# A graph layer with experts: queries kept on chip, message sums in a ring of 12 tiles, a reordered first stage

## The chip, the core and the metric

The kernel runs on one core of a Trainium2 chip. The core has a matrix engine (PE; its weight loads are listed apart as PEld), a vector engine (DVE), an activation engine (ACT), a general engine (POOL), an engine that only issues transfers (SP), and 16 DMA engines [...]. The engines run side by side, each through its own instructions in order, and wait for each other through semaphores. The metric is the time on the device in microseconds (us); lower is better. Before the change the median of three runs is 1573.82 us (1571.39 to 1576.54).

## What is computed

The input is `x` (6250 nodes of 256 numbers) and 100,000 weighted edges, sorted by destination. Everything is float32.

```python
xn = layernorm(x)
# graph convolution, residual inside
deg  = segment_sum(edge_weight, dst) + 1;  dinv = rsqrt(deg)
agg  = segment_sum((dinv[src] * edge_weight * dinv[dst])[:, None] * (xn @ W)[src], dst)
h    = agg + (dinv * dinv)[:, None] * (xn @ W) + b
gnn  = relu(0.5 * (layernorm(h) * gamma + beta) + 0.5 * xn)
# linear attention, 8 heads of 32, over all nodes
q = elu(xn @ Wq.T) + 1;  k = elu(xn @ Wk.T) + 1;  v = xn @ Wv.T
mix = (q @ (k.T @ v) / (q @ sum(k))) per head, then @ Wproj.T + bproj
x = x + gnn + mix
# 16 experts, the best 2 for each node, hidden width 512
y = layernorm(x);  gate = y @ gate_w + gate_b
w, e = softmax and index of the 2 highest gates
moe = sum_k w[k] * (relu(y @ w1[e[k]] + b1) @ w2[e[k]] + b2)
out = x + layernorm(y + moe) * f_gamma + f_beta
```

The graph sum is linear, so the kernel sums the rows of `dinv * xn` over the edges first and multiplies each sum by `W` after it.

## The kernel before

Nodes lie in 49 tiles of 128 rows; `X`, all of them, stays on chip. Edges are cut into 782 chunks of 128. `gps_layer` loads the edges and `X`, checks that the destinations of every group of eight chunks lie in a known window of 128 nodes, and branches to `windowed_layer`, which is what runs here; the other branch is not taken.

**Setup** (lines 239 to 445). Local destinations and weights, which lie as rows of edges, are transposed on PE into columns `loc_t`, `w_t` (`columns`, line 357); sources follow as `src_t`. Degrees are counted by one-hot products: for each of four quarters of the columns DVE builds `lo1` (line 396) and `hw` (line 400), and PE adds 196 small products per quarter into `deg` (line 408). DVE then takes mean and variance of the 49 tiles (lines 423 to 426), and a chain of small steps gives `dinv` and the scale and shift of the table, `rsd` and `nmr` (lines 433 to 444). The table `dinv * xn` is written to `AGG` (49 tiles on chip, line 449; ACT line 454, DVE line 456) and from there to memory as `w_hs` (lines 459, 461).

**The woven part.** All that follows is one loop over slots (line 1109). In slot c, POOL gathers the 128 source rows of chunk c from `w_hs` by an indirect DMA (line 1114) into one of 12 rows buffers, DVE builds a weighted one-hot matrix `hot` (line 1118), and PE multiplies chunk c - 6 (`LAG = 6`, line 1127); at the end of each group of eight chunks DVE adds the result to the tile's sum in `AGG` (line 1135). Between these, the slot runs pieces of other work that a class `Weave` keeps in a queue: each piece is a generator that says after how many slots it wants to go on. So the order of PE, DVE, ACT and SP is written out by the slot numbers; POOL's order is made by the planner of the tile framework. The pieces are:

- `own_terms`: each tile's own row, the table times `dinv` in place (line 663).
- `attend(t)`, one tile every 2.1 slots from slot 0: transposes of `xn` (line 474), keys (line 511), elu on ACT and DVE (lines 494 to 496), and products of keys with `xn` collected in two banks over all tiles (line 518). `context` turns them into one 256 x 256 matrix `M`.
- `zeros`: fills the slots of the expert inputs and outputs in memory (`w_xslots`, `w_yslots`, two sets of nodes) with zeros, 1 MB a transfer (line 884).
- `residual(pair of tiles)`: transposes of `xn` and of the sums, queries (line 585), `W` (line 591), the denominator, `M` (line 623), both layernorms, gates (line 655). A pair starts when its sums are complete, 16 slots after the pair before it at the earliest.
- `route(z, n)`: for 11 groups of tiles (line 118; eight of the first set, of 36 tiles, three of the second, of 13) the two best experts and a place for every token. It starts `RES` = 28 slots after the last residual piece of its group started.
- `scatter`: the normalised tokens by indirect DMAs into `w_xslots` (line 864), 98 in all.
- `expert`: 121 blocks of 128 tokens. SP loads the block's weights in two parts (642 and 512 KB) and its tokens (128 KB); PE, ACT and DVE compute (lines 936 to 965); SP stores 128 KB. Blocks start every 8, then 6 slots in the first set, every 4 in the second, not before their route; weights have four places, two of them in `AGG`.
- `combine(pair)`: two gathers per tile from `w_yslots` (line 987), the weighted sum, the last layernorm, and the output, one of five buffers `h` (line 1009). A pair every 5 slots; the first set after its last block, the second after the last block of all.

A sum's place in `AGG` is used again after its residual: as homes of tokens, weights and gathered rows (lines 1042 to 1050). One core, one SP queue: its loads, stores, fills and outputs go out in program order.

Of the kernel before, what the change touches and what calls it, by code (L numbers as in the profile page):

```python
# [122 lines left out]
RES = 28  # L123
# [8 lines left out]
def load_rows(eng, t, a):  # L132

    n = (ER - 2) * EW
    eng.dma_start(t[:ER - 2, :], a[:n].rearrange("(p c) -> p c", p=ER - 2))
    eng.dma_start(t[ER - 2:ER - 1, :], a[n:n + EW].rearrange("(p c) -> p c", p=1))
    eng.dma_start(t[ER - 1:ER, :PADC], a[n + EW:].rearrange("(p c) -> p c", p=1))

# [21 lines left out]
def gps_layer(ctx: ExitStack, tc: tile.TileContext, x, src, dst, ew, **rest):  # L160
# [8 lines left out]
    loc_e, src_e, ew_e = rows3[:ER, 0, :], rows3[:ER, 1, :].bitcast(I32), rows3[:ER, 2, :]  # L169
    flag = top.tile([1, 1], I32, name="flag")  # L170
    with tc.tile_pool(name="chk", bufs=1) as cp, \
            tc.tile_pool(name="chk_ps", bufs=1, space=bass.MemoryType.PSUM) as cps:
# [7 lines left out]
        for t0 in range(0, NFULL, 8):  # L180
# [5 lines left out]
                       allow_small_or_imprecise_dtypes=True)  # L186
        v.tensor_tensor(loc_e.rearrange("p (j e) -> p j e", j=CPR),
                        dst_e.rearrange("p (j e) -> p j e", j=CPR),
                        lo[:, :, None].to_broadcast([ER, CPR, P]), op=OP.subtract)
        ends = cp.tile([ER, 2], F32, name="ends")  # L190
# [5 lines left out]
        one = cp.tile([ER, 1], F32, name="one")  # L196
        v.memset(one, 1.0)
# [7 lines left out]
    with tc.If(ok) as cmp:  # L205
        windowed_layer(tc, X, rows3, **rest)
# [11 lines left out]
def windowed_layer(ctx: ExitStack, tc: tile.TileContext, X, rows3, W, b, gamma, beta, wqT, wkvT, wprojT, bproj,  # L218
# [4 lines left out]
    loc_e, src_e, ew_e = rows3[:ER, 0, :], rows3[:ER, 1, :].bitcast(I32), rows3[:ER, 2, :]  # L223
# [16 lines left out]
    ident = one([P, P], "ident")  # L240
    make_identity(nc, ident)
# [12 lines left out]
    zero_b = one([P, 512], "zero_b", BF)  # L254
    v.memset(zero_b, 0.0)
    ones = one([P, P], "ones")
    v.memset(ones, 1.0)
    before = one([P, P], "before")
    v.tensor_scalar(before, iota_row, iota_p, None, op0=OP.is_gt)
# [4 lines left out]
    v.tensor_scalar(tok, tok, float(N), 64.0, op0=OP.is_ge, op1=OP.mult)  # L264
    eps_t = one([P, 1], "eps_t")
    v.memset(eps_t, EPS)

# [4 lines left out]
    v.memset(mv1, 1.0)  # L272
# [3 lines left out]
    v.memset(mv2, 1.0)  # L276
# [3 lines left out]
    v.memset(logits[:, NFULL, :], 0.0)  # L280
# [3 lines left out]
    v.memset(usual, 1.0)  # L284
# [3 lines left out]
    v.memset(ones3, 1.0)  # L288
    loc_t = one([P, NCA], "loc_t")
    w_t = one([P, NCA], "w_t")  # L290
    src_t = one([P, NCA], "src_t", I32)

# [38 lines left out]
    wkv_sb = weight(wkvT, 2 * D, "wkv_sb", part(2, 2 * D))  # L331
    wq_sb = weight(wqT, D, "wq_sb")
# [9 lines left out]

    with tc.tile_pool(name="deg", bufs=1) as sp, \
            tc.tile_pool(name="deg_ps", bufs=1, space=bass.MemoryType.PSUM) as sps:
        spread = sp.tile([16, 8, P], F32, name="spread")
        v.memset(spread, 0.0)
        for a in range(8):
            v.tensor_copy(spread[:, a, a * 16:(a + 1) * 16], ident[:16, :16])
# [7 lines left out]

        def columns(rows_e, outs):
            for h in range(2):
                tp = sps.tile([P, CPR // 2, ER], F32, name="tpe", bufs=2)
                for j in range(CPR // 2):  # L360
                    c0 = (h * CPR // 2 + j) * P
                    nc.tensor.transpose(tp[:, j, :], rows_e[:, c0:c0 + P], ident[:ER, :ER])
                for o, copy in outs:
                    copy(o.rearrange("e (p j) -> e j p", j=CPR)[:, h * CPR // 2:(h + 1) * CPR // 2, :], tp)

        columns(loc_e, [(loc_i, v.tensor_copy), (loc_t, nc.scalar.copy)])
        columns(ew_e, [(w_t, nc.scalar.copy)])
# [20 lines left out]

        deg = sps.tile([16, 3, 512], F32, name="deg")
# [3 lines left out]
        for c0 in range(0, NCA, C):  # L393
# [26 lines left out]
        for t in range(NT):  # L420
# [3 lines left out]
            if t:  # L424
                v.bn_aggr(mv1[:, t - 1, :], halves[t - 1])
# [1239 lines left out]
```

## Time and profile before

| | us |
|---|---|
| median of 3 runs | 1573.82 |
| the profiled execution | 1570.62 |
| its span, first to last instruction | 1568.8 |
| busy: PE, DVE, POOL, ACT | 1302.3, 1023.2, 959.7, 610.6 |
| granted PE clock, mean | 0.948 |
| moved by DMA | 360.96 MB, 230 GB/s on average |

The span has stages with different limits. Gathers start at 115.8 and the last one at 1232.0; the first combine's work on DVE starts at 1326, PE's last block ends about 1502, and the rest is the combines of the second set. A page line of section 5 gives a group of like instructions: how many, busy time and mean length of one, then the idle time of the engine just before them and what ended most of it. A line of the window view gives busy time and instruction count of each engine in a stretch. PE's instructions overlap in time, so starts, not lengths, say what one costs. DMA-issuing instructions of POOL count here as busy[...].

### The profile page before, as it was taken

What the parts mean: (1) busy time and instruction counts of PE and PEld (TensorE: products, weight loads), DVE (VectorE), ACT (ScalarE), POOL (GpSimd) and SP (SyncE); (2) the same over time, 40 slices, a digit from 0 to 9 for tenths busy, and PEclk for the clock granted to TensorE, in tenths of its full rate; (3) what the DMA queues carried; (4) which work ended last, traced back from release to release, by engine and by line L of the source; (5) the groups of instructions that cost most, each with busy time, mean ns of one, the idle gap of its engine ahead of it and who ended that gap; (6) DMA issues with size and microseconds to landing.
All of it is one profiled execution on the core that took longest, in us unless ns stands there. A gap on an engine that the chain in (4) does not pass through costs nothing.

```text
span 1568.8 us, 23681 instructions
## 1 busy us (share of the span) xinstructions
PE 1302.3 (83%) x6438; PEld 972.2 (62%) x6438; DVE 1023.2 (65%) x3578; ACT 610.6 (39%) x1542; POOL 959.7 (61%) x990
## 2 busy tenths in 40 slices
PE   2918999887678989899998989979999987878930
PEld 2817888565456767677675767757767754545620
DVE  7953345578664877758577685856685756889045
ACT  1044555454422424234342433423433443455421
POOL 0007777777777777777777777777777404752042
PEclk9999999999789999999998998989999998999975
DMA  8059993333356767678776757668877767999932
GB/s 235 2 205 374 385 372 99 104 104 104 115 195 215 252 214 252 213 265 270 254 252 208 249 177 255 220 226 267 273 251 253 245 203 261 360 382 345 364 112 71
DMA packets 173553, 360.96 MB, mean 230 GB/s; under 512 B 26305, under 2 KB 110604, under 8 KB 173402
## 3 DMA queue, kind: packets, MB, share of 16 engines
q1 hardware_dynamic: 125454, 230.28, 42.1%
q0 software_dynamic: 47712, 128.17, 25.8%
q8 instruction: 57, 0.93, 0.3%
q10 hardware_dynamic: 236, 0.80, 0.2%
q14 instruction: 94, 0.77, 0.2%
HBM read 283.60 MB, written 75.54 MB: 229 GB/s over the span
## 4 chain that ended last, share of the span: by engine, by line


## 5 line engine op out<-in xcount | busy, mean ns | idle before, releaser
L1114 POOL DMA_INDIRECT rows<-w_hs,src_t x782 | 759.1, 971 | 349.2 <-issue 183.3
L1127 PE MATMUL acc<-rows,hot 128*128 128x256 f32 x1564 | 473.2, 407 | 72.3 <-DMA rows<-w_hs,src_t 64.5
L1127 PEld LDWEIGHTS acc<-rows,hot 128*128 128x128 f32 x1564 | 271.9, 198 | 138.2 <-issue 43.3
L1118 DVE TENSOR_SCALAR hot<-iota_g,loc_t,w_t 128x128 f32<-128x128 f32 x782 | 255.7, 356 | 25.9 <-PE acc L1127 25.9
L987 POOL DMA_INDIRECT AGG<-w_yslots,slot_i x98 | 99.5, 1015 | 125.7 <-DMA w_yslots<-AGG 82.6
L864 POOL DMA_INDIRECT w_xslots<-AGG,slot_i x98 | 99.5, 1015 | 97.7 <-ACT AGG L940 51.2
L957 ACT ACTIVATE hT<-htp,early 128x128 f32<-128x128 f32 x300 | 85.7, 369 | 175.3 <-PE htp L952 141.8
L944 PE MATMUL hp<-early,AGG 128*128 128x512 f32 x300 | 145.7, 609 | 9.4 <-ACT AGG L940 8.5
L961 PE MATMUL yp<-early,hT 128*128 128x256 f32 x600 | 146.3, 388 | 1.4 <-ACT hT L957 1.2
L496 DVE SCALAR_TENSOR_TENSOR q<-e,q 128x256 f32<-128x256 f32 (+1 forms) x98 | 41.9, 427 | 146.4 <-ACT q L495 144.2
L961 PEld LDWEIGHTS yp<-early,hT 128*128 128x128 f32 x600 | 116.7, 196 | 28.8 <-ACT hT L957 7.8
L948 DVE COPY AGG<-hp 128x512 f32<-128x512 f32 x92 | 63.3, 688 | 86.1 <-PE hp L944 85.9
L944 PE MATMUL hp<-AGG 128*128 128x512 f32 x184 | 89.9, 611 | 8.2 <-ACT AGG L940 7.2
L952 PE MATMUL htp<-ident,AGG 128*128 128x128 f32 x484 | 75.4, 279 | 20.3 <-DVE AGG L948 13.8
L961 PE MATMUL yp<-AGG,hT 128*128 128x256 f32 x368 | 88.4, 383 | 0.8 <-ACT hT L957 0.8
L944 PEld LDWEIGHTS hp<-early,AGG 128*128 128x128 f32 x300 | 55.9, 192 | 53.3 <-issue 36.7
L302 ACT ACTIVATE sd<-mv,eps_t 128x2 f32<-128x2 f32 (+2 forms) x76 | 22.5, 297 | 168.9 <-DVE mv L297 133.3
L961 PEld LDWEIGHTS yp<-AGG,hT 128*128 128x128 f32 x368 | 69.8, 192 | 21.6 <-ACT hT L957 7.2
L957 ACT ACTIVATE hT<-htp,AGG 128x128 f32<-128x128 f32 x184 | 52.4, 367 | 69.9 <-PE htp L952 46.2
L952 PEld LDWEIGHTS htp<-ident,AGG 128*128 128x128 f32 x484 | 58.9, 143 | 33.4 <-DVE AGG L948 17.4
L1135 DVE SCALAR_TENSOR_TENSOR AGG<-acc,dinv,AGG 64x256 f32<-64x256 f32 x147 | 70.8, 482 | 11.5 <-PE acc L1127 8.5
L965 DVE TENSOR_TENSOR AGG<-yp,early 128x256 f32<-128x256 f32 x75 | 31.7, 422 | 68.2 <-PE yp L961 60.6
(259 smaller groups left out, 2144.7 us busy)
## 6 DMA issues: line engine op xcount, KB each, us to landing
early<-in_experts SPq DMA_DIRECT2D x75, 642.0 KB
early<-in_experts SPq DMA_DIRECT2D x75, 512.0 KB
AGG<-in_experts SPq DMA_DIRECT2D x46, 642.0 KB
AGG<-in_experts SPq DMA_DIRECT2D x46, 512.0 KB
w_xslots<-zero_b SPq DMA_DIRECT2D x16, 1024.0 KB
w_yslots<-zero_b SPq DMA_DIRECT2D x16, 1024.0 KB
AGG<-w_xslots SPq DMA_DIRECT2D x121, 128.0 KB
w_yslots<-AGG SPq DMA_DIRECT2D x121, 128.0 KB
```

Source lines behind the costliest of these rows:

```text
L496: v.scalar_tensor_tensor(q[:r], e[:r], 1.0, q[:r], op0=OP.min, op1=OP.add)
L864: i = nc.gpsimd.indirect_dma_start(out=xslots[z], out_offset=IndirectOffsetOnAxis(ap=slot_i[:r, t, k:k + 1], axis=0), in_=y[:r], in_offset ...
L944: nc.tensor.matmul(hp, xT[:, c, :], w1[:, c, :], start=(c == 0), stop=(c == 1))
L948: copy_h(h, hp)
L952: nc.tensor.transpose(tp[:, f, :], h[:, f * P:(f + 1) * P], ident)
L957: act(hT[:, f, :], tp[:, f, :], AF.Relu, bias=b1[:, f:f + 1], scale=1.0)
L961: nc.tensor.matmul(yp[:, :D], hT[:, f, :], w2[:, f, :], start=(f == 0), stop=(f == FJ - 1))
L987: nc.gpsimd.indirect_dma_start(out=got[i, k]()[:r], out_offset=None, in_=yslots[z], in_offset=IndirectOffsetOnAxis(ap=slot_i[:r, t, k:k + ...
L1114: nc.gpsimd.indirect_dma_start(out=hrows[c], out_offset=None, in_=hs, in_offset=IndirectOffsetOnAxis(ap=src_t[:, c:c + 1], axis=0))
L1118: v.tensor_scalar(hots[c], iota_g[:, group_of(c) % 2, :], loc_t[:, c:c + 1], w_t[:, c:c + 1], op0=OP.is_equal, op1=OP.mult)
L1127: nc.tensor.matmul(accs[g], hots.pop(c), hrows.pop(c), start=begin, stop=end)
L1135: v.scalar_tensor_tensor(AGG[p0:p1, t, :], acc[p0:p1, :], dinv[p0:p1, t:t + 1], AGG[p0:p1, t, :], op0=OP.mult, op1=OP.add)
```

## The change

**Queries with the keys.** `attend` multiplies `xn` by keys and queries in one 512-wide product, and the elu of both is done 512 wide on ACT. The queries stay on chip in `Q`, 49 tiles, which first hold the table on its way to memory. `residual` no longer makes queries nor transposes `xn`; it works on both tiles of a pair at once where it can.

**Sums in a ring.** `AGG` of 49 tiles is gone. A sum lives in one of 12 places: the first four tiles in the two `hT` buffers, the others in a ring of eight. `own_term(t)` reads the tile's table rows back from `w_hs` and scales them; it runs for one tile at a time, as places come free.

**First stage.** `ident`, `loc_t` and `w_t` move into `gps_layer`, ahead of the branch, and that block is ordered by hand. Memsets of constants move behind the one-hot loops (`constants`). The first quarter of the one-hot loop is cut in two. For 32 tiles ACT makes the sums for mean and variance (`two_sums`), DVE keeps 17. The fill of the first `w_xslots` moves ahead of the table. The table is written in 14 slots before slot 0, between the first attends.

**The schedule.** Attends start at slot -14, 2.3 slots apart before slot 0 and 3.6 after; residual pairs may follow at 10 slots; `RES` is 24; the last 30 blocks of the first set come every 5 slots; the other fills (`fill`, the old `zeros`) come every 8. The output of `combine` has three buffers, shared by name with other rows. By these rules the last residual piece starts at slot 791 (before 797), the last route at 815 (825), the first combine at 815 (831), the last expert block at 941 (965), and the combines of the second set at 959 (983).

The diff, cut to its core:

```diff
-RES = 28
+RES = 24
...
+def columns(nc, pool, ident, rows_e, o):
+    for h in range(2):
+        tp = pool.tile([P, CPR // 2, ER], F32, name="tpe", bufs=2)
+        for j in range(CPR // 2):
+            c0 = (h * CPR // 2 + j) * P
+            nc.tensor.transpose(tp[:, j, :], rows_e[:, c0:c0 + P], ident[:ER, :ER])
+        nc.scalar.copy(o.rearrange("e (p j) -> e j p", j=CPR)[:, h * CPR // 2:(h + 1) * CPR // 2, :], tp)
...
+            tc.tile_pool(name="chk_ps", bufs=1, space=bass.MemoryType.PSUM) as cps, by_hand(tc):
...
+        make_identity(nc, ident)
+        one = cp.tile([ER, 1], F32, name="one")
+        v.memset(one, 1.0)
+        scratch = cp.tile([ER, 1], F32, name="scratch")
+        nc.scalar.copy(scratch, one)
         v.tensor_tensor(loc_e.rearrange("p (j e) -> p j e", j=CPR),
                         dst_e.rearrange("p (j e) -> p j e", j=CPR),
                         lo[:, :, None].to_broadcast([ER, CPR, P]), op=OP.subtract)
+        columns(nc, cps, ident, loc_e, loc_t)
+        columns(nc, cps, ident, ew_e, w_t)
...
+    def constants():
+        v.memset(ones, 1.0)
+        v.tensor_scalar(before, iota_row, iota_p, None, op0=OP.is_gt)
+        v.tensor_scalar(tok, tok, float(N), 64.0, op0=OP.is_ge, op1=OP.mult)
+        v.memset(eps_t, EPS)
+        v.memset(mv1[:, NFULL, :], 1.0)
+        v.memset(mv2, 1.0)
+        v.memset(logits[:, NFULL, :], 0.0)
+        v.memset(usual, 1.0)
+        v.memset(ones3, 1.0)
...
+    wkq = part(2, 2 * D)
+    weight(wkvT[:, :D], D, "wk", wkq[:, :, :D])
+    weight(wqT, D, "wq", wkq[:, :, D:])
+    wv = weight(wkvT[:, D:], D, "wv", part(2, D))
...
+    for _ in fill(0, xslots[0]):
+        pass
...
+        v.tensor_copy(loc_i, loc_t)
...
+        def two_sums():
+            for t0 in range(0, SA, 8):
+                for t in range(t0, t0 + 8):
+                    act(sp.tile([P, D], F32, name="unread", bufs=2), X[:, t, :], AF.Identity,
+                        accum_out=sums_[:, t:t + 1])
+                act(minus[:, t0:t0 + 8], sums_[:, t0:t0 + 8], AF.Identity, scale=-1.0 / D)
+                for t in range(t0, t0 + 8):
+                    act(sp.tile([P, D], F32, name="unread", bufs=2), X[:, t, :], AF.Square,
+                        bias=minus[:, t:t + 1], accum_out=squares[:, t:t + 1])
...
+        for n in (C // 2, C // 2, C, C, C):
...
+                columns(nc, sps, ident, sf, src_t)
+                two_sums()
+            c0 += n
...
+        for t in range(SA, NT):
...
+    def table(t):
+        r = rows(t)
+        if t % 4 == 1:
+            act(Q[:r, t, :], X[:r, t, :], AF.Identity, bias=nmr[:r, t:t + 1], scale=rsd[:r, t:t + 1])
+        else:
+            v.tensor_scalar(Q[:r, t, :], X[:r, t, :], mv1[:r, t, 0:1], rsd[:r, t:t + 1],
+                            op0=OP.subtract, op1=OP.mult)
+        if t % TG == TG - 1:
+            t0 = t + 1 - TG
+            n = min(NFULL, t0 + TG) - t0
+            nc.sync.dma_start(hs[t0 * P:(t0 + n) * P, :].rearrange("(t p) c -> p t c", p=P), Q[:, t0:t0 + n, :])
+            if n < TG:
+                nc.sync.dma_start(hs[NFULL * P:, :], Q[:rows(NFULL), NFULL, :])
...
+        kq = bank("kq")
         for k in range(2):
-            nc.tensor.matmul(kp[:r, :D], xnT[:, k, :r], wkv_sb[:, k, :D], start=(k == 0), stop=(k == 1))
-        kf = mp.tile([P, D], F32, name="q", bufs=3)
-        elu1(kf, mp.tile([P, D], F32, name="e", bufs=2), kp[:r, :D])
+            nc.tensor.matmul(kq[:r], xnT[:, k, :r], wkq[:, k, :], start=(k == 0), stop=(k == 1))
+        e = mp.tile([P, 2, D], F32, name="two_a", bufs=2)
+        pos = mp.tile([P, 2, D], F32, name="two_b", bufs=2)
+        act(e[:r].rearrange("p a c -> p (a c)"), kq[:r], AF.Exp)
+        act(pos[:r].rearrange("p a c -> p (a c)"), kq[:r], AF.Relu)
+        kf = mp.tile([P, D], F32, name="row", bufs=3)
+        v.scalar_tensor_tensor(kf[:r], e[:r, 0, :], 1.0, pos[:r, 0, :], op0=OP.min, op1=OP.add)
+        v.scalar_tensor_tensor(Q[:r, t, :], e[:r, 1, :], 1.0, pos[:r, 1, :], op0=OP.min, op1=OP.add)
...
+    RING = 8
+    hTs = [wp.tile([P, F], F32, name=f"hT{j}") for j in range(2)]
+    ring = [wp.tile([P, D], F32, name=f"agg{j}") for j in range(RING)]
+    def agg(t):
+        return hTs[t // 2][:, t % 2 * D:(t % 2 + 1) * D] if t < 4 else ring[(t - 4) % RING]
+    begun, summed, read = set(), set(), set()
+    def own_term(t):
+        r = rows(t)
+        nc.sync.dma_start(agg(t)[:r], hs[t * P:t * P + r, :])
+        yield 4
+        nc.scalar.mul(agg(t)[:r], agg(t)[:r], dinv[:r, t:t + 1])
+        begun.add(t)
...
+        q8 = q.rearrange("p t c -> p (t c)").rearrange("p (h d) -> p h d", d=HEAD)
+        qk = two("qk", 1)
+        v.tensor_tensor(qk[:r0], q, ksum[:r0, None, :].to_broadcast([r0, n, D]), op=OP.mult)
+        den = mp.tile([P, 16], F32, name="den", bufs=2)[:r0, :8 * n]
+        v.tensor_reduce(den, qk[:r0].rearrange("p t (h d) -> p t h d", d=HEAD).rearrange("p t h d -> p (t h) d"),
+                        axis=AX.X, op=OP.add)
+        yield 1
+        v.tensor_scalar(den, den, 1e-6, None, op0=OP.max)
+        v.reciprocal(den, den)
+        v.tensor_mul(q8, q8, den[:, :, None].to_broadcast([r0, 8 * n, HEAD]))
...
+        agT = turned([agg(t)[:r0] for t in ts_], "two_a", 2)
+        for t in ts_:
+            summed.add(t)
+        yield 3
+        hp = bank("hp").rearrange("p (t c) -> p t c", t=2)
+        for i in range(n):
+            for k in range(2):
+                nc.tensor.matmul(hp[:r0, i, :], agT[:, k, i * P:i * P + r0], w_sb[:, k, :], start=(k == 0), stop=False)
+            add_bias(hp[:r0, i, :], 0)
+        h = two("h2", 2)
+        nc.scalar.copy(h[:r0], hp[:r0, :n, :])
...
+        qT = turned([Q[:r0, t, :] for t in ts_], "two_b", 2)
+        for t in ts_:
             read.add(t)
...
+            o = pool.tile([P, D], F32, name="row", bufs=3)
...
+    PRE = 14
+    at = -PRE
     for t in range(NT):
-        weave.add(int(pitch * t), attend(t))
-    at = int(pitch * NT) + 9
+        weave.add(int(at), attend(t))
+        at += 2.3 if at < 0 else 3.6
...
+    to_fill = [(0, yslots[0]), (1, xslots[1]), (1, yslots[1])]
+    fill_at = 4
+    for z, a in to_fill:
+        weave.add(fill_at, fill(z, a))
+        fill_at += 8 * ((MOST[z] + 8) // 8)
+    summed_at = {}
+    def sum_from(t):
+        weave.add(max(16 * t - 4, summed_at.get(t - RING, -4) + 1 if t >= 4 + RING else -4), own_term(t))
+    for t in range(4 + RING):
+        sum_from(t)
...
+                for t in range(t0, t1):
+                    summed_at[t] = at + 3
+                    if t + RING < NT and t >= 4:
+                        sum_from(t + RING)
+                at += 10
...
+            ready = max(last_at + RES, scattered - 2)
...
+            scattered = ready + 11 + 2 * (b - a) * slow
...
-                block = max(block + (4 if z else 8 if n < 3 else 6), ready)
+                block = max(block + (4 if z else 8 if n < 3 else 5 if flush else 6), ready)
...
+    slot = -PRE
     while slot < NCH + LAG or weave.steps:
+        for t in range(NT * (slot + PRE) // PRE, NT * (slot + PRE + 1) // PRE if slot < 0 else 0):
+            table(t)
         c = slot
-        if c < NCH:
+        if 0 <= c < NCH:
...
+                        v.scalar_tensor_tensor(agg(t)[p0:p1], acc[p0:p1, :], dinv[p0:p1, t:t + 1], agg(t)[p0:p1],
```

## The prediction

> **What bounds the kernel now.** I read the page first, then busy time by stage, then single engines in order of time. Page: busy tenths of POOL and DMA, and the costliest group.
>
> ```profile
> POOL 0007777777777777777777777777777404752042
> ...
> DMA  8059993333356767678776757668877767999932
> ...
> L1114 POOL DMA_INDIRECT rows<-w_hs,src_t x782 | 759.1, 971 | 349.2 <-issue 183.3
> ```
>
> POOL shows a steady 7 from slice 4 to 30; it is full, as its timeline shows (start, length, idle before it):
>
> ```profile
> 352.98 0.94 POOL L1114 DMA_INDIRECT rows<-w_hs,src_t  x1 [0.30 <-issue]
> 354.23 0.94 POOL L1114 DMA_INDIRECT rows<-w_hs,src_t  x1 [0.30 <-issue]
> ...
> 1257.54 0.96 POOL L864 DMA_INDIRECT w_xslots<-AGG,slot_i  x1 [0.30 <-issue]
> 1309.68 0.96 POOL L864 DMA_INDIRECT w_xslots<-AGG,slot_i  x1 [51.18 <-ACT AGG L940]
> ```
>
> 0.94 of work and 0.30 between: 1.25 us for every indirect DMA. Counting gathers in this view, gather 0 starts at 115.8, gather 639 at 1030.9 and 781, the last, at 1232.0. Up to gather 639 there are 72 scatters too, so 711 DMAs in 915.1 us, 1.287 us each. That stretch is POOL's. Busy time of PE, PEld, DVE, ACT, POOL by stage, then clock, DMA share, GB/s:
>
> ```profile
> 83.00:116.00 33.00, 6.83 (x24) 5.41 (x24) 18.16 (x75) 15.59 (x33) 0.19 (x1) 1.00 0.66 227
> ...
> 1031.00:1244.00 213.00, 202.90 (x944) 152.56 (x943) 137.13 (x462) 81.58 (x216) 151.00 (x155) 0.98 0.79 262
> 1244.00:1326.00 82.00, 64.38 (x267) 41.91 (x265) 46.20 (x184) 34.29 (x90) 20.49 (x20) 0.94 0.69 233
> 1326.00:1452.00 126.00, 106.22 (x405) 67.26 (x406) 111.65 (x306) 62.83 (x181) 66.66 (x66) 0.96 0.97 350
> 1452.00:1502.00 50.00, 49.12 (x205) 33.03 (x204) 4.67 (x11) 23.70 (x67) 0.00 (x0) 1.00 0.85 311
> 1502.00:1569.00 67.00, 3.09 (x16) 2.17 (x14) 38.49 (x108) 10.01 (x24) 27.02 (x26) 0.56 0.29 83
> ```
>
> From 1031 to 1244 PE and POOL are about equally full. 1244 to 1326 is full nowhere. From 1326 DVE and DMA are full (first combines), then PE (last blocks), then DVE (last combines). PE's timeline there gives the price of an expert block:
>
> ```profile
> 1458.04 0.38 PE L936 MATMUL xtp<-ident,AGG 128*128 128x128 f32 x2
> 1458.26 0.60 PE L952 MATMUL htp<-ident,AGG 128*128 128x128 f32 x4
> 1458.94 1.98 PE L944 MATMUL hp<-AGG 128*128 128x512 f32 x4
> 1460.76 1.89 PE L961 MATMUL yp<-early,hT 128*128 128x256 f32 x8
> 1462.48 0.38 PE L936 MATMUL xtp<-ident,AGG 128*128 128x128 f32 x2
> ```
>
> From start to start 4.44 us. The starts also price single matmuls: 1.82 for four of 512 columns, 0.215 for one of 256, 0.11 for one of 128. The setup before gather 0, in order of time:
>
> ```profile
> 73.55 1.44 PE L417 MATMUL deg<-zero_b 128*16 128x504 bf16 x3
> ...
> 92.66 9.46 DVE L456 TENSOR_SCALAR AGG<-X,mv,rsd 128x256 f32<-128x256 f32 x29
> ...
> 115.81 1.12 POOL L1114 DMA_INDIRECT rows<-w_hs,src_t  x1 [103.20 <-issue]
> ```
>
> [...]
>
> **Part 1, setup.** Edge transposes before the branch: loc_e is ready at 7.1; ACT needs 8.0 (its sixth DMA issue ends at 6.5, table load 1.28), four copies of 0.8 end at 11.2; the flag's matmul waits on PE behind the fourth group: flag some 0.9 late. In exchange DVE reaches the one-hot loops at 17.8 (0.57 cast, four of 0.28, 3.8 for the thirds, from 12.3) instead of 25.4. Two half chunks cost 5.8 each (16 x 0.10 + 24 x 0.174, half of the elements, same fixed part) for one of 8.6; so chunk 2 ends at 38.0. Then PE's 196 small matmuls are the bound, 9.64 each: 38.0 + 3 x 9.64 + 1.44 = 68.3 (before 75.0). DVE now has 17 instead of 49 row statistics: four chunks end at 56.3, constants 1.2, bias thirds 2.7, 17 x 0.39: 67.2. ACT's 64 sums start after src_t at 30.9: [...] I take under 68. Then as before deg sums, dps and dinv: 1.94 + 5.0 (87.7 to 92.75), nmr at 75.3 instead of 92.75: 17.4 gained.
> The table stage: before 23.1 from nmr to gather 0. Now 14 slots with the first attends among the tables: par and memsets first 1.4, 37 x 0.33 on DVE, four attends' 8 x 0.43, waits for ACT's Exp and Relu about 2: last store issued at 19.5, landing and start 6 (before, 106.3 to 115.8 behind more traffic): 25.5. **Gather 0 at 101, gain 15.** The 11 fills of the first xslots (1 MB per 2.8 us) run from 31 to 64 in an idle DMA: nothing.
>
> **Part 2, slots 0 to 635.** POOL's count of DMAs is the same: 1.287 each. Attends: PE 0.22 + 1.72 + 0.86 per 3.6 slots plus 0.43 = 1.21 per slot, under POOL's. Without that cover (fewer slots) it would be PE's. Slots 171 to 237, residual pairs every 10 slots: before a pair cost DVE 9.8 (51.6 busy in 312 to 376, less 0.42 per slot, 3.1 pairs); five pairs of 256-wide operations become 512-wide, two elu go: about 8.2, so 1.24 per slot with hot and sums, just under. LAG leaves six slots of cover. The 49 table reads (128 KB, 6.4 MB in all) lie beside DMA at 0.65 to 0.7; ACT waits if one lands later than four slots, 5 us, and behind it stand ACT's copies of xT and hT, for which PE waits. On SP a read waits for PE to have turned the ring tile's last content, three slots earlier in the order, and expert loads stand behind it. I take 0, from -5 to +12.
>
> **Part 3, slots 635 to 788.** PE: 153 x 0.43 + 29 blocks x 4.11 (starts in PE's timeline from 1110 on, without waits: yp 1.73, hp 1.72, htp 0.44, xtp 0.22) + 10 tiles x 3.35 (three pairs of transposes 0.66, hp and mix with bias 1.16 each, gl 0.37; before 4.43, with qp 0.86 and a fourth pair) + 2 for routes = 221. The same sum for before gives 217 where 213 passed, so 216 against 218.5 (1025 to 1243.5): **-2.5**. Spacing 5 instead of 6 means that 29 of 30 blocks of the first set are done or under way, not 26.
>
> **Part 4, slots 788 to the first combine.** By the schedule's arithmetic the last residual moves from slot 797 to 791, its route from 825 to 815, the combines from 831 to 815, the last block's load from 965 to 941. Before: 82.5 us from 1243.5 to the first combine's DVE work at 1326: PE work 46, 12 of waits, and then POOL: five scatters of the last route stood ahead of the first combine gathers, at 1309.7 to 1314.7, landing at 1326. In the changed kernel's order 15 combine gathers stand ahead of those six scatters, and the stores they read are issued at slot 796. So: 5 blocks and three tiles, 31, the same 12, five slots 6: 49. **-33**. What is late next is the last scatter, behind one freed gather tile; the blocks that need it load from slot 829.
>
> **Part 5, to PE's end.** Before: 18 combine pairs of DVE 6.7 us (five slots, 1.34 per slot) to slot 926, then 1.11 per slot (4.44 / 4) to 978: 179 by this sum, 176 measured. Now 90 x 1.34 + 44 x 1.11 = 170, and the last route's DVE work (some 5) falls inside. DMA: 31 loads x 1.41 MB + 14 MB in 172 us is 335 GB/s, under the 350 measured. **-4.** Ring of three output rows instead of five: DVE reuses one after 10 us; an output queued behind one block's 1.15 MB at 350 GB/s lands in some 5. Hidden; without that up to 20. **Last 67 us unchanged.**
>
> Sum: -15 + 0 - 2.5 - 33 - 4 = -54.5 against the profiled 1570.6 (span 1568.8), which lies 3.2 below the median of 1573.8: **1519 us.**
>
> **Rivals.** (a) The combines start earlier but the tail does not shrink: DMA at 0.97 and DVE at 89% already fill 1326 to 1502, and the last scatters now queue behind gathers. For it: those shares; against: 2 to 3 fewer loads left. Then Part 4 gives some 12 and Part 5 nothing: 1545. (b) Part 1's ACT sums, or tables mixed with attends, eat the setup's gain and the rest holds: 1534. (c) The middle gains too, since fills hold DMA for 60 us instead of 90 and PE is lighter: at 1.26 per DMA 711 x 0.027 = 19 less, 1500, and down to 1490 with the tail's stalls. (d) Slower: ACT waits in order for each tile's table read. 49 reads; from 59 / 49 = 1.2 us lost to POOL at each, all gain is gone; at 1.3 us it is 1519 + 64 = 1583. Against: six slots of cover, DMA at 0.65. That the change does nothing is no rival: slots and counts differ in the built order.
>
> **Chances.** Forecast 0.55 (its own range 1502 to 1536), (a) 0.25, (b) within the forecast's upper edge 0.05, (c) 0.08, no change 0.02, (d) 0.05. A measurement of this kernel tells 0.3%. Faster 0.93, same 0.02, slower 0.05. The range leaves out (d), the far end of (a) and half of (c): 1496 to 1556.
>
> **What would show it.** nmr near 75 and gather 0 near 101; gather 635 near 1010; the last gather near 1225; combine gathers ahead of the last six scatters, DVE's first combine near 1274; PE's last block near 1447. Wrong if ACT shows waits on the ring's tiles of several us, if accumulating ACTIVATEs take over 0.6 us, or if PE idles in the last blocks.

## The result, and the profile after

The changed kernel takes 1549.3 us (1545.9 to 1551.4) beside 1575.2 us (1571.4 to 1579.0) for the kernel before, ratio 0.983, 95% interval 0.980 to 0.986: 26 us faster, where 54.5 were forecast. The time lies inside the widest range given (1496 to 1556) and outside the forecast's own (1502 to 1536). The profiled spans are 1547.3 and 1568.8, 21.5 apart, since the profiled execution of the kernel before, 1570.6, lay ahead of its median. From the gathers in POOL's timelines and from PE's last block, by stretch:

| stretch | before | after | forecast | measured |
|---|---|---|---|---|
| span's start to gather 0 | 115.8 | 107.6 | -15 | -8.2 |
| gather 0 to 635 | 907.7 | 915.4 | 0 | +7.7 |
| gather 635 to 781, the last | 208.5 | 220.3 | -2.5 | +11.8 |
| gather 781 to PE's end | 273.6 | 240.9 | -37 | -32.7 |
| PE's end to the span's end | 63.2 | 63.1 | 0 | -0.1 |

The forecast cut the third and the fourth stretch at slot 788, which is where PE's last product of gathered rows ends: 1243.7 before, 1260.5 after. Cut there, the third measures +17.3 (220.2 to 237.5) and the fourth -38.2 (261.9 to 223.7). So the setup fell short by 7 us, the next stretch by 8, the third by 20, and the fourth came as forecast. The page of the changed kernel, busy tenths and the gathers' group:

```profile
POOL 1017777777777777777777777777667734753042
...
DMA  9789933333345766677887878768878868899932
...
L1163 POOL DMA_INDIRECT rows<-w_hs,src_t x782 | 762.2, 975 | 354.1 <-ACT two_a L552 89.7
```

POOL's row of sevens is as long as before, but has two sixes in it (slices of 38.7 us, 1083 to 1161 us), where it had none: POOL waits there. Its timeline: gather 0, the first combine gather, the last two combine gathers ahead of the last route's scatters, and the first and last of those:

```profile
107.56 1.15 POOL L1163 DMA_INDIRECT rows<-w_hs,src_t  x1 [89.72 <-ACT two_a L552]
...
1280.83 0.98 POOL L1025 DMA_INDIRECT Q<-w_yslots,slot_i  x1 [10.29 <-DMA w_yslots<-Q]
...
1310.09 1.07 POOL L1025 DMA_INDIRECT Q<-w_yslots,slot_i  x1 [4.61 <-DVE xn L1036]
1311.47 0.95 POOL L1025 DMA_INDIRECT Q<-w_yslots,slot_i  x1 [0.30 <-DVE over L845]
1313.71 1.00 POOL L911 DMA_INDIRECT w_xslots<-Q,slot_i  x1 [1.29 <-issue]
...
1320.86 1.59 POOL L911 DMA_INDIRECT w_xslots<-Q,slot_i  x1 [0.30 <-issue]
```

The order is the one forecast: 15 combine gathers ahead of six scatters. Busy time by stage of the changed kernel (PE, PEld, DVE, ACT, POOL, then clock, DMA share, GB/s):

```profile
1023.00:1243.00 220.00, 207.84 (x940) 153.88 (x940) 128.38 (x399) 65.41 (x193) 153.36 (x158) 0.98 0.84 284
1243.00:1484.00 241.00, 210.96 (x850) 138.70 (x848) 165.45 (x523) 112.46 (x322) 88.41 (x87) 0.96 0.86 309
...
1325.00:1430.00 105.00, 86.03 (x327) 55.31 (x326) 94.02 (x260) 52.79 (x153) 55.94 (x56) 0.95 1.00 369
1430.00:1485.00 55.00, 52.77 (x219) 35.25 (x217) 12.07 (x32) 26.87 (x76) 0.00 (x0) 1.00 0.79 283
```

And the kernel before, over the same two stretches (gather 635 to 781, and on to PE's end):

```profile
1023.50:1232.00 208.50, 195.37 (x898) 145.44 (x896) 133.69 (x434) 73.96 (x197) 156.04 (x160) 0.98 0.78 260
1232.00:1505.00 273.00, 234.21 (x953) 154.12 (x952) 173.67 (x553) 130.25 (x361) 88.08 (x87) 0.96 0.84 300
```

Add the two rows of each kernel, and call PE's busy time its work and the rest its waits: PE has 429.6 us of work in 481.5 before, 418.8 in 461 after. The 20.5 us gained from gather 635 to PE's end are 10.8 of work, from the lighter residuals (their queries' products, busy for 11.4 us there before, are gone), and 10 of waits. What else the rows show is that work changed sides: the first stretch got 12 us of PE more, the second 23 less. In the first stretch PE's yp matmuls, eight to a block, count 168 before (21 blocks) and 208 after (26).

### The profile page after: what moved, and what is told of

It reads as the page before. It is cut to its first block, busy times and chain, and to the rows that moved or that the text cites. A ratio compares the mean times of both kernels' runs of the same rounds, so it can differ in the third digit from the quotient of the medians.

```text
span 1547.3 us, 22816 instructions
## 1 busy us (share of the span) xinstructions
PE 1312.2 (85%) x6144; PEld 930.1 (60%) x6144; DVE 975.0 (63%) x3338; ACT 530.6 (34%) x1417; POOL 967.1 (63%) x999
## 5 line engine op out<-in xcount | busy, mean ns | idle before, releaser
L1025 POOL DMA_INDIRECT Q<-w_yslots,slot_i x98 | 99.4, 1015 | 141.8 <-issue 81.1
L994 ACT ACTIVATE hT<-htp,early 128x128 f32<-128x128 f32 x296 | 84.5, 368 | 205.6 <-issue 130.1
L981 PE MATMUL hp<-early,Q 128*128 128x512 f32 x296 | 143.2, 607 | 5.6 <-ACT Q L977 4.7
L998 PEld LDWEIGHTS yp<-early,hT 128*128 128x128 f32 x592 | 116.9, 198 | 32.7 <-ACT hT L994 10.8
L985 DVE COPY Q<-hp 128x512 f32<-128x512 f32 x92 | 63.4, 689 | 113.7 <-PE hp L981 113.0
L911 POOL DMA_INDIRECT w_xslots<-Q,slot_i x98 | 99.6, 1016 | 46.8 <-issue 37.1
L549 PE MATMUL kq<-early,xnT 128*128 128x512 f32 (+1 forms) x196 | 98.5, 627 | 4.3 <-ACT xnT L545 4.3
L981 PE MATMUL hp<-Q 128*128 128x512 f32 x188 | 92.4, 615 | 10.1 <-ACT Q L977 9.1
L989 PE MATMUL htp<-ident,Q 128*128 128x128 f32 x484 | 74.7, 278 | 21.4 <-DVE Q L985 17.8
L998 PE MATMUL yp<-Q,hT 128*128 128x256 f32 x376 | 91.6, 388 | 0.4 <-ACT hT L994 0.3
L998 PEld LDWEIGHTS yp<-Q,hT 128*128 128x128 f32 x376 | 72.9, 195 | 19.6 <-ACT hT L994 5.2
L1185 DVE SCALAR_TENSOR_TENSOR agg<-acc,dinv,agg 64x256 f32<-64x256 f32 x135 | 65.0, 482 | 28.6 <-PE acc L1176 25.9
```

Source lines behind the costliest of these rows:

```text
L549: nc.tensor.matmul(kq[:r], xnT[:, k, :r], wkq[:, k, :], start=(k == 0), stop=(k == 1))
L911: i = nc.gpsimd.indirect_dma_start(out=xslots[z], out_offset=IndirectOffsetOnAxis(ap=slot_i[:r, t, k:k + 1], axis=0), in_=y[:r], in_offset ...
L981: nc.tensor.matmul(hp, xT[:, c, :], w1[:, c, :], start=(c == 0), stop=(c == 1))
L985: copy_h(h, hp)
L989: nc.tensor.transpose(tp[:, f, :], h[:, f * P:(f + 1) * P], ident)
L994: act(hT[:, f, :], tp[:, f, :], AF.Relu, bias=b1[:, f:f + 1], scale=1.0)
```

## The experiments

In the table the times are medians, the ratio is to the kernel before on the same chip; stretches are from one profiled run each, as above (that of e2 was the fastest of its four runs, 1555.5, that of e8 the slowest of its 18, 1575.3). Each text set off below was written ahead of its run.

| kernel | us | ratio (95%) | gather 0 | 0 to 635 | 635 to 781 | 781 to PE's end |
|---|---|---|---|---|---|---|
| e1_old_schedule | 1554.1 | 0.987 (0.985 to 0.990) | 107.4 | 909.9 | 204.3 | 266.5 |
| e2_flush6 | 1559.5 | 0.992 (0.990 to 0.993) | 106.0 | 914.6 | 203.0 | 266.2 |
| e3_warm | 1544.7 | 0.981 (0.979 to 0.983) | 103.3 | 915.6 | 218.6 | 241.5 |
| e4_spread | 1537.6 | 0.978 (0.975 to 0.982) | 106.1 | 914.1 | 220.1 | 234.1 |
| e5_stats_dve | 1558.3 | 0.990 (0.987 to 0.993) | 117.0 | 911.3 | 220.4 | 243.4 |
| e6_no_mix | 1541.3 | 0.980 (0.976 to 0.984) | 101.8 | 914.2 | 218.9 | 242.1 |
| e7_warm_spread8 | 1531.7 | 0.972 (0.969 to 0.976) | 104.3 | 915.0 | 220.3 | 228.1 |
| e8_before_flush5 | 1568.9 | 0.997 (0.996 to 0.998) | 116.3 | 906.7 | 222.4 | 265.3 |
| d1_res28 | 1550.0 | 0.985 (0.982 to 0.987) | 108.1 | 912.6 | 217.3 | 247.3 |
| d2_no_mix_spread8 | 1528.4 | 0.971 (0.969 to 0.973) | 102.2 | 912.4 | 220.3 | 226.6 |

**What the schedule is worth.** Two theories: the slots set the time (as the prediction reckoned), or PE's work and its waits do, whichever side of the last gather a block falls on. First both numbers of the schedule back:

```
-RES = 24
+RES = 28
...
-    ... 8 if n < 3 else 5 if flush else 6), ready)
+    ... 8 if n < 3 else 6), ready)
```

> The changed kernel with two numbers of the schedule as before: RES 28 instead of 24, 6 slots instead of 5 between the blocks of the first set's last phase. By the slot arithmetic the first combines go back from slot 815 to 831 and the last block's load from 941 to 965, as in the kernel before; all else stays. Theory W (from gather 635 to PE's end the time is PE's work, 421 us in the changed kernel and 430 before, plus what PE waits, 40 and 50; the schedule only decides on which side of the last gather a block falls): gather 635 to 781 goes back from 220 to about 208, the stretch after it grows by about as much, and the whole is 6 to 14 us slower than the changed kernel, 1555 to 1563. Theory S (the prediction's Parts 4 and 5: the 37 us are due to the earlier slots): the whole is 30 to 37 us slower, 1579 to 1586.

Then the spacing alone (the second of these edits):

> The changed kernel with only the spacing of the first set's last blocks back at 6 slots. The first combines start at slot 827 instead of 815, the last block's load at 961 instead of 941. Theory W: PE's five blocks are taken out of the stretch between gather 635 and 781, which shrinks from 220 to 207 to 210, and put behind it; the whole moves by less than 6 us, 1545 to 1555. Theory S: the combines start 12 slots later and the whole is 20 to 25 us slower, 1570 to 1575. Both expect six scatters of the last route ahead of all combine gathers again.

And the spacing alone in the kernel before, the other way round (6 to 5):

> The kernel before with one number changed: 5 instead of 6 slots between the blocks of the first set's last phase. The first combines move from slot 831 to 825, the last block's load from 965 to about 951. Theory W (PE's work and waits): about five blocks more fall between gather 635 and 781, which takes 8 to 14 us longer, and the stretch behind it gets shorter by that and up to 8 us more: 1566 to 1575 against 1574. Theory S (the slots set the time): 12 to 20 us faster than before. Rival: slower by 3 to 8 us, since the combines' gathers collide with more loads.

Undone, the two cost 5 us (e1) and the spacing alone 10 (e2), not the 30 and more of the slot theory. e1's 5 is just under its range of 6 to 14; e2's 10 is outside of the 6 expected, on the side of the slot theory but half of it. That e1, which undoes more, loses less goes with its shorter way to gather 635 (909.9 us). Set alone into the kernel before, the spacing gains 5 (inside the range of work and waits), and lengthens 635 to 781 by 14 there, as it shortens it by 16 and 17 when it is taken out: that stretch follows the number of blocks in it. The stages of e1:

```profile
1017.00:1222.00 205.00, 190.27 (x852) 140.44 (x851) 121.63 (x379) 58.64 (x165) 154.85 (x161) 0.97 0.80 270
1222.00:1488.00 266.00, 226.55 (x933) 149.22 (x931) 171.04 (x540) 120.94 (x348) 88.34 (x87) 0.97 0.86 308
```

416.8 of work in 471: the work of the changed kernel with the waits (54) of the kernel before. What the waits are, the first combine shows. In the kernel before, in e1 and in e2 the last route's scatters stand ahead of the first combine gathers on POOL; DVE, in order, waits for those gathers, and PE for DVE. DVE's first combine in the kernel before and in e1, then PE's waits for DVE behind gather 781 in the kernel before, in e1 and in the changed kernel (us in total, times, the longest):

```profile
1321.23 1.00 DVE L998 SCALAR_TENSOR_TENSOR xn<-AGG,w,xn 128x256 f32<-128x256 f32 x2 [9.59 <-DMA AGG<-w_yslots,slot_i]
1305.05 0.49 DVE L1036 SCALAR_TENSOR_TENSOR xn<-Q,w,xn 128x256 f32<-128x256 f32 x1 [9.71 <-DMA Q<-w_yslots,slot_i]
...
PE htp L952 <- DVE AGG L948: 13.8, 8, 8.8
PE htp L989 <- DVE Q L985: 19.3, 11, 9.9
PE htp L989 <- DVE Q L985: 6.6, 3, 2.8
```

So the combine gathers that come ahead of the scatters are worth the 10 us of waits, and the residuals' edits the other half of the gain.

**The waits that are left.** If DVE holds PE while it does the first combines, stretching them over the blocks behind should free PE:

```
-        at += 5
+        at += 7 if t0 < CUT else 5
```

> The changed kernel with 7 instead of 5 slots between the combine pairs of the first set (their end at slot 934 instead of 900, still ahead of the second set's combines at 959). Theory: between 1281 and 1430 DVE is at 125 of 149 us with combines and makes PE wait some 25 us (for Q from ACT and DVE), while from 1430 to 1485 DVE has 12 of 55 and PE 53: spread over the blocks, DVE no longer holds PE, PE's end moves from 1484 to 1466 to 1476, the whole is 8 to 18 us faster, 1531 to 1541. Rival 1: that stage is DMA's (share 1.00 from 1325 to 1430), so PE waits for its loads anyway: within 4 us. Rival 2: later combines keep the x and got tiles longer and end behind the last block: slower by 3 to 10 us.

12 us faster than the changed kernel; PE ends at 1474.3, within the range. PE's work stays (417.5 in 454.1 from gather 635 on), its waits fall from 42 to 37, and the stretch behind gather 781 loses 7 of the 12; most of the rest lies ahead of gather 781, where the edit does nothing and executions differ. With 8 slots and an attend-free table stage (d2_no_mix_spread8, below) the stage in which DMA had a share of 1.00 reads:

```profile
1325.00:1430.00 105.00, 99.37 (x402) 65.57 (x402) 72.22 (x200) 59.31 (x167) 45.77 (x48) 0.99 1.03 397
```

PE 99 instead of 86, DVE 72 instead of 94, and DMA moves 397 instead of 369 GB/s: a share of 1.00 was not the most that it moves. (This kernel is 8 us ahead; eight us earlier, from 1317, it reads 96, 72 and 388.) Spreading the combines moves their transfers too, so the edit alone doesn't part DVE from DMA. The waits from 1281 to 1430 do, first those of the changed kernel, then those of d2:

```profile
ACT sd L318 <- DVE mv L313: 38.9, 17, 6.2
PE hp L981 <- ACT Q L977: 11.1, 9, 2.2
PE xtp L973 <- DMA Q<-w_xslots: 1.0, 1, 1.0
...
ACT sd L318 <- DVE mv L1017: 8.5, 9, 1.4
PE hp L981 <- ACT Q L977: 3.1, 7, 0.8
```

In the changed kernel PE waits 1.0 us for a transfer. It waits for ACT's copies of the blocks' tokens, and ACT, in order, for DVE's statistics in the combines. So DVE holds PE, in part through ACT, and the DMA half of rival (a) falls.

**The setup.** PE's timeline of the changed kernel among the tables: attends 0, 1 and 2.

```profile
78.72 0.69 PE L518 MATMUL tp<-ident,early 128*128 128x128 f32 x2 [2.64 <-ACT early L540]
79.96 3.78 PE L549 MATMUL kq<-early,xnT 128*128 128x512 f32 x4 [0.55 <-ACT xnT L545]
83.53 0.63 PE L518 MATMUL tp<-ident,early 128*128 128x128 f32 x2
85.66 3.78 PE L549 MATMUL kq<-early,xnT 128*128 128x512 f32 x4 [1.50 <-ACT xnT L545]
...
90.89 1.98 PE L549 MATMUL kq<-early,xnT 128*128 128x512 f32 x4 [0.29 <-ACT xnT L545]
```

The first two kq (keys and queries) take 3.78 us, the third 1.98: the first two, with idle times of 2.64 and 0.55 us and of 1.50 us just before them, ran at about half rate. DVE stands behind them, its remaining tables behind each attend's sums:

```profile
84.89 0.42 DVE L555 SCALAR_TENSOR_TENSOR row<-two_a,two_b 128x256 f32<-128x256 f32 x1 [1.83 <-ACT two_b L553]
...
90.60 0.42 DVE L555 SCALAR_TENSOR_TENSOR row<-two_a,two_b 128x256 f32<-128x256 f32 x1 [1.78 <-ACT two_b L553]
```

Three experiments: PE kept busy ahead of them (heat(n) is n bf16 matmuls of 512 columns on zeros, whose result nobody reads), no attend among the tables at all, and the sums on ACT undone.

```
+        heat(4)
         dps = sps.tile(...)
...
+        heat(8)
         act(sdeg, dps, AF.Sqrt, ...)
```

> The changed kernel with 12 extra bf16 matmuls of 512 columns on zeros whose result nobody reads: 4 ahead of the degree sums' transposition, in PE's idle 70.4 to 72.4, and 8 behind it, in its idle 76.1 to 78.7. In the changed kernel the first two attends' four kq matmuls take 3.78 us each instead of the 1.98 of the later ones. Theory: PE runs at half rate after idling, and this holds the tables back, because the tables stand behind the attends on DVE: kq at about 2.0 to 2.6 in both, gather 0 at 104 to 106 instead of 107.6, the whole 2 to 3.5 us faster. Rival: the table stage is held by the stores' landing or by ACT: gather 0 within 0.7 us of 107.6, the whole unchanged.

```
-    at = -PRE
+    at = 0
...
-        at += 2.3 if at < 0 else 3.6
+        at += 3.15
```

> The changed kernel with no attend among the tables: all 49 start from slot 0 on, every 3.15 slots, so that the last one and the residuals come in the same slots as before. Tables alone: DVE 37 x 0.33 from 78.7 on, last store issued near 92, gather 0 at 97 to 100 (107.6 in the changed kernel). Theory: then PE sets slots 0 to 155, (0.22 + 1.82 + 0.86 + 3.15 x 0.43) / 3.15 = 1.35 us per slot instead of POOL's 1.26: gather 150 at about 300 to 306 against some 300 in the changed kernel, so that nothing is left of the earlier start: the whole from 2 us faster to 8 us slower. Rival: POOL holds its 1.26 us and the whole gains what gather 0 gains, 8 to 10 us.

```
-                two_sums()
...
-        for t in range(SA, NT):
+        for t in range(NT):
...
-        v.tensor_scalar(mv1[:, :SA, 0], minus, ...)
-        v.tensor_scalar(mv1[:, :SA, 1], squares, ...)
```

> The changed kernel without the sums on ACT: all 49 row statistics on DVE again, 0.39 us each, 32 more than in the changed kernel, 12.5 us. DVE reaches the degree sums at about 79.9 instead of 70.5 (2.9 us of the 12.5 go into its wait for PE there), so nmr at 86 to 87 instead of 77.2 and gather 0 at 116 to 118. Theory: POOL is full from gather 0 to 635, so the setup carries through one to one: the whole 8 to 11 us slower than the changed kernel, 1557 to 1561. Rival: the attends' matmuls, not POOL, set the first 160 slots, and absorb half of it: the whole 3 to 6 us slower.

With PE busy both kq take 1.98 and gather 0 comes at 103.3:

```profile
79.06 1.98 PE L549 MATMUL kq<-early,xnT 128*128 128x512 f32 x4 [0.80 <-ACT xnT L545]
80.88 0.38 PE L518 MATMUL tp<-ident,early 128*128 128x128 f32 x2
83.20 1.98 PE L549 MATMUL kq<-early,xnT 128*128 128x512 f32 x4 [1.94 <-ACT xnT L545]
```

That is 4.3 us ahead of the changed kernel and 2.7 ahead of e2 and e4, which have the changed kernel's setup unaltered (e7, with the same extra matmuls, has 104.3); the whole is 4.6 faster, though the intervals (0.979 to 0.983 and 0.980 to 0.986) still touch. Without attends among the tables gather 0 comes at 101.8 (97 to 100 expected) and the whole is 8 us faster. Here my expectation was wrong and its rival right: PE was to set 1.35 us per slot from then on, but gathers 100 to 200 came every 1.32, scarcely slower than in the changed kernel (132.5 us instead of 131.8), so little was given back. The sums on ACT are worth 9 us, as much as the whole gain of the setup: without them gather 0 is at 117.0, later than in the kernel before, and of these 9.4 us 9.0 are left at the end. The theory was right.

**Both ends together:**

> The extra matmuls of e3_warm and the first combines every 8 slots (e4_spread had 7) together. The two act at the two ends of the kernel; if they add up, 1.5 to 4.6 us of the first and 10 to 14 of the second: 1530 to 1537. If 8 slots are one too many, because the second set's gathers then wait behind the first set's last ones: 1537 to 1545.

> The changed kernel with e6_no_mix and 8 slots between the first combines together. e6_no_mix was 8 us faster than the changed kernel and the spacing 12 to 13 (e4_spread, e7_warm_spread8 less e3_warm); they act at different ends, so if they add up 1527 to 1532, and if not 1533 to 1540.

> Attends from slot 0 on and 8 slots between the first combines, a third time. Beside the changed kernel on the second chip it was 29 us faster. Where the kernel before takes 1574: 1525 to 1532, ratio 0.969 to 0.974.

d2_no_mix_spread8 is e6_no_mix with 8 slots between the first combines: 1528.4 us, 21 faster than the changed kernel and 46 than the one before. The 8 of e6 and the 13 between e3 and e7 (the same matmuls without and with 8 slots) make 21: they add up. e7's own 1531.7 lies in its first range. Eight slots alone were not run. e10 is the same kernel as d2, on another chip (below).

**The 7.7 us before gather 635.** They sit in two places: gathers 200 to 300 took 162.9 us instead of 157.6, and 500 to 635 207.3 instead of 203.3. For the second the routes' position was suspected, for the first the residuals' spacing:

```
-RES = 24
+RES = 28
```

```
-                at += 10
+                at += 10 if t0 < 4 else 14
```

> The changed kernel with RES 28 instead of 24 alone: every route, its scatters and blocks four slots later after its residuals, the first combines at slot 819 instead of 815. From gather 0 to 635 e1_old_schedule (RES 28) took 909.9 us, e2_flush6 (RES 24) 914.6, the changed kernel 915.4, the kernel before 907.7. Theory: the earlier routes put their DVE chains right behind the residuals', PE waits for them and then runs at half rate, and that is some 5 of the 7.7 us that the changed kernel lost before gather 635: 909 to 911 here, the whole 3 to 6 us faster than the changed kernel. Rival: the four slots come back in the tail as 4 to 5 us, the whole within 2 us.

> The same with RES 28. If the routes' position is worth what e9_res28 is to show, 3 to 6 us faster than e10_no_mix_spread8, 1522 to 1528; if it comes back in the tail, within 2 us of it.

> The changed kernel with 14 instead of 10 slots between the residual pairs from the third on, where they catch up with the gathers (slots 191 to 240; before: 16). Theory: DVE at 0.9 to 0.95 there lengthens POOL's own DMAs (mean of gathers 200 to 249 1.025 us in the changed kernel, 0.971 before): the mean falls to 0.96 to 0.99, gather 200 to 300 takes 158 to 160 instead of 162.9, the whole 2 to 4 us faster. Rival: it is the route behind them, not their spacing: no change within 1.5 us.

These, and e10_no_mix_spread8, landed on a chip on which the kernel before itself took 1780 us, so their times can't be set against the runs above. Repeated with the changed kernel beside them:

> The changed kernel itself, as the measure for the three beside it, since the last four ran where the kernel before took 1780 us instead of 1574. If the chip is like the first one: 1545 to 1553 against 1571 to 1577, gather 0 to 635 in 914 to 916 us.

> RES 28 alone in the changed kernel, once more. Theory (the earlier routes cost PE waits before gather 635): gather 0 to 635 in 909 to 911, the whole 3 to 6 us faster than c1_after. Rival: the four slots come back in the tail, within 2 us.

> 14 instead of 10 slots between the residual pairs from the third on, once more. Theory: mean of gathers 200 to 249 falls from 1.025 to 0.96 to 0.99 us, gather 200 to 300 takes 158 to 160, the whole 2 to 4 us faster than c1_after. Rival: within 1.5 us.

> Attends from slot 0 on and 8 slots between the first combines, once more. If the two add up 19 to 22 us faster than c1_after, 1527 to 1532; if not 1533 to 1540.

This was again a chip of that kind (1782 us before). Ratios there: e9 0.994, e10 0.983, e11 0.986, e12 0.995 on the one; c1 0.995 (0.993 to 0.997), c2 0.993 (0.989 to 0.997), c3 0.991 (0.987 to 0.995), c4 0.982 (0.977 to 0.986) on the other. POOL is not full there: gather 0 to 635 takes 1075 us in c1_after, and POOL's waits read

```profile
POOL rows L1163 <- PE acc L1176: 174.5, 149, 8.9
POOL rows L1163 <- issue: 142.2, 451, 1.7
```

where the changed kernel on the first chip has

```profile
POOL rows L1163 <- PE acc L1176: 76.0, 188, 5.2
```

So on such a chip the change gains 0.5% instead of 1.7%, and c4_no_mix_spread8 1.4% more than the change (29 us, where 19 to 22 were expected); why these chips are slower the profiles don't say. For both edits, RES 28 and the 14 slots, these chips give no verdict. With 14 slots the mean of gathers 200 to 249 is 0.992 us (c3) and 0.977 (e12), with 10 slots 0.996 to 1.008 (c1, c2, c4, e10, e11): shorter, but POOL is not full there, so the time need not follow. With RES 28 e11 is 8 us slower than e10 and c2 4.5 faster than c1, within their intervals. c3 is 9 us faster than c1, more than either of its theories has, and their intervals overlap too. RES alone once more, on another chip:

> RES 28 alone in the changed kernel, a third time, in the hope of a chip on which the kernel before takes some 1574 us. Theory: gather 0 to 635 in 909 to 911 us (changed kernel 915.4), gather 500 to 635 in 203 to 205 (207.3), the whole 1543 to 1546. Rival: the four slots come back in the tail, 1547 to 1551, or gather 0 to 635 stays at 914 to 916.

It landed on a chip like the first. Gathers 500 to 635 take 204.5 us there and 203.9 in e1, both with RES 28, and 205.6 to 208.1 in the changed kernel and the seven others with RES 24 on such chips: some three of the 7.7 us go with the routes' position, and 1.3 of them only because one scatter more of the route falls ahead of gather 635 (159 of POOL's DMAs instead of 158). Gather 0 to 635 took 912.6, between the two ranges. But the whole is 1550.0: from gather 781 to PE's end it takes 247.3 us instead of 240.9, and what was gained ahead of it is gone. The rival was right.

## Why the prediction was wrong

**Part 1, -15 against -8.2.** The order of the setup came as worked out: flag and one-hot loops early, PE's small matmuls the bound, the sums on ACT hidden behind them (30 us from 32.2 to 62.4, where they were taken to end under 68), the half chunks at 5.6 us each instead of 5.8 (0.100 and 0.174 us an instruction, the full ones 0.126 and 0.276). nmr came at 77.2 instead of 75.3, since the one-hot loops began at 19.2 instead of 17.8. The step that failed is the table stage: 30.4 us instead of 25.5. It had about 2 us for DVE's waits on ACT's Exp and Relu in the four attends ahead of the last table; these waits were 5.8 (1.83, 1.78 and two of 1.10), since each attend is a chain through PE, ACT and DVE, the first two with PE at half rate (kq 3.78 instead of 1.98). So the last store was issued 23.2 us after nmr instead of 19.5, and from it to gather 0 passed 7.2 instead of 6. With PE kept busy the stage is 27.0 in e3 and 28.6 in e7, and without any attend 24.7 (e6: nmr 77.1, gather 0 101.8). The number 101 would have been right for tables alone.

**Part 2, 0 against +7.7.** Within the range given (-5 to +12), wrongly centred. The wait on the ring's table reads (rival d) did not occur: ACT's group of ring tiles shows, as idle time before it in the whole run,

```profile
  DMA agg<-w_hs: 1.2, 2
```

1.2 us, twice. What cost was named as "just under": DVE at 1.24 of POOL's 1.287 in the dense residuals. There POOL's own DMAs got longer: the 124 of gathers 200 to 300 took 124.6 us instead of 119.8, 4.8 of the 5.3 us lost, so waits of POOL were hardly longer there. DVE was busy 19.0 of 20 us in 380 to 400, and the traces have long gathers beside a busy DVE: from gather 100 to 635 of the changed kernel those with DVE busy for 95% of them or more take 1.019 us (but the 80 among these with 98% or more take 0.975), those with DVE busy for less than a quarter 0.951. That DVE is the cause is argued, not shown: the run meant to lighten it (14 slots) gave no verdict. From 500 to 635 it is one scatter more, 1.3, and 2.7 of waits for PE.

**Part 3, -2.5 against +11.8 (+17.3 at its own cut): the largest miss.** The step that failed is how two sums of PE's work became times. The stretch from gather 635 to the end of PE's last product of gathered rows, in the changed kernel and in the one before:

```profile
1023.00:1260.50 237.50, 224.03 (x1010) 165.51 (x1009) 141.99 (x459) 70.71 (x207) 154.31 (x159) 0.99 0.82 278
1023.50:1243.70 220.20, 207.07 (x961) 155.12 (x960) 144.15 (x484) 81.28 (x216) 156.97 (x160) 0.98 0.78 259
```

The sum for the changed kernel, 221, was near the 224.0 measured. The one for the kernel before, 217, was 10 too high: it had 25.5 blocks, and 22 ran (in the changed kernel 28, with 29 in the sum). And 13 us of waits come on top of the work in either kernel. The working left them out and took 5 us off as well: it scaled 221 by 213 over 217, but 213 us is the stretch from 1031 to 1244, and set the result, 216, against 218.5, the stretch from 1025. So 17 us more of work became 2.5 less of time. The work is that of the blocks that the spacing of 5 slots brought ahead of this point: six at 4.11 are 25 us, against 11 saved on ten tiles (4.43 less 3.35 each), 14 of the 17. e2 and e8 show that the blocks do it, with the spacing alone. PE's clock is not the reason: 0.99 and 0.98 were granted.

**Parts 4 and 5, -37 against -32.7 (-38.2 at their own cut): right, mechanism included.** The order of combine gathers and scatters came as worked out, and DVE's wait of 9.6 us for the gathers went. From PE's last product to the first combine on DVE it was 77.5 us before (that combine began at 1321.2, not at the 1326 of the working) and 41.9 after: -35.6, forecast -33. From there to PE's end it was 184.4 (PE's end is 1505.6, not 1502) and 181.8: -2.6, forecast -4. The first combine came at 1302 instead of 1274 and PE's end at 1484 instead of 1447 for what Parts 1 to 3 had lost ahead of them. But the -38 is in large part the reverse of Part 3's +17: blocks that ran earlier are not there any more. Together they are worth 20.9, half of it waits.

**The rivals.** Rival (a)'s number, 1545, was the nearest, by luck: the stretch that it doubted shrank as forecast, and the loss lay ahead of it. That DVE, not DMA, fills the first combines is so (e4). Rival (b) held in part, by 7 us of setup, without its consequence that the rest holds. (c) and (d) did not come; (d)'s 59 us should have been the 54.5 of the gain, 1.1 us for each read.

## What to carry to other kernels

If one engine is nearly full through several stages, add its work and its waits over all of them before pricing an edit stage by stage: work moved ahead of a boundary is a loss on one side of it and most of the gain on the other. And test a sum of work on the kernel before: what is left between it and the time there is waits, which stay (13 us here, in either kernel), or a wrong count. In a stage with two things at full share (DVE and DMA here), what the third engine waits for tells which of them holds it (PE: 1.0 us for a transfer); spreading that one's work over the stage behind is a one-number edit, and gave 12 us. And filling a short stage with first pieces of later work (attends among the tables) is free only if no engine must take the two in turn (this stage took 30.4 us with them and 24.7 without).

## What the runs showed of the hardware

PE's half rate was in no step of the forecast. In the setup the same four kq matmuls took 3.78 us twice, behind idle times of 0.55 to 2.64 us, and then 1.98; with e3's extra matmuls ahead of them they took 1.98 every time. It came again in a full stage: at 1138.7, for 2.4 us, PE waits for DVE, and then yp takes 3.62 instead of 1.89 and hp 2.48 instead of 1.88, some 5 us at half rate:

```profile
1141.11 0.61 PE L792 MATMUL tots<-cnt,ones 128*128 128x16 f32 x2 [2.37 <-DVE cnt L783]
...
1142.97 3.62 PE L998 MATMUL yp<-early,hT 128*128 128x256 f32 x8
1146.38 2.48 PE L981 MATMUL hp<-Q 128*128 128x512 f32 x4
```

The length of the wait alone does not decide it: after one of 3.2 us, which ended at 1166.2, yp took 1.99 and hp 1.88, and in e3 the second kq took 1.98 after an idle time of 1.94. What does decide it the runs don't show. The clock column reads 0.50 from 1142 to 1146, but 1.00 from 79 to 91, where kq took double: there the half rate is seen only in the matmuls' durations.

An ACTIVATE that also sums is two instructions on ACT here: the second starts 0.31 us after the first, and the next ACTIVATE 0.09 us after that, so a sum costs 0.40 us (0.49 for the sums of squares, L420), under the 0.6 named in the prediction:

```profile
32.65 0.41 ACT L416 ACTIVATE unread<-X 128x256 f32<-128x256 f32 x1
32.96 0.19 ACT L416 ACTIVATION_READ_ACCUMULATOR unread<-X 128x1 f32 x1
33.05 0.41 ACT L416 ACTIVATE unread<-X 128x256 f32<-128x256 f32 x1
```
